# Row e of a convolution layer, spread over the partitions by GpSimd instead of by TensorE

## The chip, the cores and the metric

The kernel runs on one core of one Trainium2 chip. The metric is the device time of one execution in microseconds (us), lower is better. The engines are named as in the profile: PE is TensorE (PEld its weight loads), DVE is VectorE, ACT is ScalarE, POOL is GpSimd, SP is SyncE, which here only issues DMAs (its queue is written SPq). L1531 is line 1531 of the kernel.

## The reference

Four residual layers act in turn on an array x of 1 x 256 x 256 x 128 (height, width, channels), all in float32, each on a group-normalised x. Layer 0 is attention over rows, layers 1 and 2 are triangle multiplications, layer 3, the last, is a pair of reversible convolution blocks. Only layer 3 matters here:

```python
DN = ('NHWC', 'HWIO', 'NHWC')
def c1(t):                       # 1 x 9 taps, 128 channels -> 1 channel
    return lax.conv_general_dilated(t, w1, (1, 1), 'SAME', dimension_numbers=DN) + b1
def c2(t):                       # 128 x 128 product at each place
    return jnp.einsum('bhwc,cd->bhwd', t, w2[0, 4]) + b2
t = relu(c1(x))
y = concatenate([x[:, :1], x[:, 1:] + t[:, :-1]], axis=1)
u = relu(c1(y))
z_main = u + roll(y, 1, axis=1)
z = concatenate([z_main[:, :H-2], u[:, H-1:H] + y[:, H-2:H-1], y[:, H-1:H]], axis=1)
v = relu(c2(z))
p = concatenate([z[:, :, :1], z[:, :, 1:] + v[:, :, :-1]], axis=2)
r = relu(c2(p))
q = r + roll(p, 1, axis=2)       # with the last two columns exchanged
out = x + q
```

The first convolution c1 has one output channel. So t and u are images of 256 x 256 without channels, and z is the normalised x, moved by one row, plus an image e = u + t (moved by one row) that is the same for all 128 channels. The normalisation is r3 * x + k0 with one factor r3 and one offset k0 a channel.

## The kernel before

Data lie with channels on the 128 partitions. Layers 0 to 2 end at about 2944 us of the execution and leave x in DRAM as `x3T`. The convolution stage follows and goes in 32 steps `s` of R = 8 image rows (2048 columns, SC), with lists of work in an order written out by hand: each engine does its instructions in that order, and so does SP's DMA queue.

The image e is made ahead of the steps, by small transfers through DRAM, in 16 blocks `b` of 16 image rows (two steps):

- `taps` (L1454, L1458, L1463): six steps ahead (LEAD), TensorE multiplies x by the nine tap columns into PSUM, ScalarE copies them to `p9_st`, and four DMAs store them as nine rows of the DRAM array sD.
- `load_block` (L1473): two DMAs load the nine shifted tap rows back with the block spread over 128 partitions, one image row on 8 of them.
- `sum_taps` and `image_u` (L1493 to L1514): VectorE sums the taps to t, and forms u from t. `keep_t` (L1499) stores t to DRAM; `load_t` (L1503) loads it moved by one image row.
- `image_e` (L1519, L1521): VectorE adds u and the moved t to e, and SP stores e to DRAM (eD).
- `load_e` (L1531): four DMAs of 4 KB load e for the block's two steps into one of two tiles `p9_er`: chunk c of 512 columns goes to partition 32c for the even step and to partition 32c + 1 for the odd one.

A step `s` of the main work then is:

- `start_z(s)` (L1541): ScalarE writes r3 * x + k0, moved by one row, to the tile `p9_z` in SBUF, in one instruction of 256 columns and one of 1792.
- `finish_z(s)` (L1082, L1555): `broadcast_rows` lets TensorE multiply each chunk of row e (32 partitions) by a selector column repeated 128 times, so that all 128 partitions of two PSUM tiles hold e. VectorE adds each half (1024 columns) to z in place.
- `p_half` (L1561, L1569): TensorE multiplies z by the 128 x 128 weights, and VectorE adds the rectified product to z, giving p (`p9_pb`).
- `q_half` (L1561, L1583, L1586): the same for p, giving q. `residual` (L1575 to L1577): GpSimd adds p, moved by one column, to q, which ScalarE started as x (L1660).
- `emit` (L1598 to L1600): TensorE turns q back to tokens, ScalarE copies it from PSUM, and SP stores it.

The steps overlap. In one turn of the loop SP issues the x load of step s + 8, in odd turns the load of t and in even turns the load of e (for steps s + 2 and s + 3); then come p of step s, z of step s + 1, q of step s - 1, the residual sum of s, the image work (even turns: taps summed and t stored; odd turns: e formed and stored, then the next taps loaded), the taps of step s + 6 and the output of step s - 2. TensorE's order in a turn is therefore: product of z(s), selector products for z(s + 1), product of p(s - 1), taps of s + 6, transposes of s - 2.

PSUM is full: two tiles of two banks for the products (`p9_pm`) and two of two banks (tag "x") which the taps, the spread e and the transposes take in turn.

Of the kernel before, what the change touches and what calls it, by code (L numbers as in the profile page):

```python
# [2 lines left out]

# [5 lines left out]

F32 = mybir.dt.float32  # L10
AF = mybir.ActivationFunctionType
ALU = mybir.AluOpType
# [4 lines left out]
P = 128  # L17
N = 256
D = 128
T = N * N  # L20
SC = 2048
NSC = T // SC
CK = 512
# [9 lines left out]
def kernel(ctx: ExitStack, tc: tile.TileContext, a: dict, out: bass.AP):  # L33
    nc = tc.nc
# [28 lines left out]
    NP = N + 8  # L63
# [5 lines left out]
    eD = dram.tile([1, N * NP], F32, name="eD")  # L69
# [168 lines left out]
    with tc.tile_pool(name="x0", bufs=1) as xres, tc.tile_pool(name="p0", bufs=3) as sb:  # L238
        held = {s: xres.tile([P, SC], F32, name=f"x0_{s}") for s in range(RES, NSC)}
        with tc.tile_pool(name="p0ps", bufs=3, space=PSUM) as ps, tc.tile_pool(  # L240
            name="f0ps", bufs=2, space=PSUM
# [167 lines left out]
        with tc.tile_pool(name="p1", bufs=2) as wk_sb, tc.tile_pool(  # L409
            name="p1ps", bufs=4, space=PSUM  # L410
# [70 lines left out]
    with tc.tile_pool(name="p2e", bufs=6) as eb, tc.tile_pool(name="p2c", bufs=1) as cs:  # L481
        triT = cs.tile([P, NH, 2, N], F32, name="triT")
        with tc.tile_pool(name="p2", bufs=2) as sb, tc.tile_pool(
            name="p2S", bufs=2, space=PSUM
        ) as psS, tc.tile_pool(name="p2z", bufs=1, space=PSUM) as psZ, tc.tile_pool(
            name="p2M", bufs=3, space=PSUM
# [302 lines left out]
    xs = {}  # L789
# [58 lines left out]
    with x1_scope:  # L848
        with tc.tile_pool(name="p3", bufs=3) as sb, tc.tile_pool(
            name="p3ps", bufs=3, space=PSUM  # L850
# [41 lines left out]
        with tc.tile_pool(name="z", bufs=2) as sb, tc.tile_pool(  # L892
            name="zps", bufs=3, space=PSUM
# [21 lines left out]
            def turn_z(k):  # L915
                if k < 16:
                    return tri_turn(nc, ps, sb, AB[k // 2][0], k % 2, ident, nc.scalar.copy)
# [4 lines left out]
            at = turn_z(0)  # L922
            for k in range(16):
                nxt = turn_z(k + 1)
                pz = tri_multiply(nc, ps, at, AB[k // 2][1], k % 2).rearrange("p t n -> p (t n)")
                at = nxt
# [32 lines left out]
        with tc.tile_pool(name="p4", bufs=3) as sb, tc.tile_pool(  # L959
            name="p4psg", bufs=2, space=PSUM  # L960
        ) as psg, tc.tile_pool(name="p4psz", bufs=2, space=PSUM) as psz, tc.manual_schedule():
            zs, gts, sums = {}, {}, []
# [42 lines left out]
            for i, s in enumerate(order):  # L1005
# [14 lines left out]
                for h in range(2):  # L1020
                    hs = slice(h * 2 * CK, (h + 1) * 2 * CK)
# [5 lines left out]
                if i in by_dve:  # L1027
                    for h in range(2):
                        hs = slice(h * 2 * CK, (h + 1) * 2 * CK)
# [47 lines left out]
    def broadcast_rows(psX, rows, s, name, tag="x"):  # L1077


        rb = [psX.tile([P, 2, CK], F32, name=name, tag=tag) for _ in range(2)]  # L1080
        for c in range(4):
            nc.tensor.matmul(  # L1082
                rb[c // 2][:, c % 2, :], lhsT=sel[32 * c : 32 * c + 32, s : s + 1].to_broadcast([32, P]),
                rhs=rows[32 * c : 32 * c + 32, :], start=True, stop=True,
            )
        return [t.rearrange("p c t -> p (c t)") for t in rb]
# [9 lines left out]
    with tc.tile_pool(name="x5", bufs=7) as x5_pool, tc.tile_pool(name="p5", bufs=2) as sb, tc.tile_pool(  # L1096
        name="p5q", bufs=4
    ) as sq_pool, tc.tile_pool(name="p5psX", bufs=1, space=PSUM) as psX, tc.tile_pool(
        name="p5psM", bufs=3, space=PSUM
    ) as psM, tc.manual_schedule():  # L1100
        xs, sqs, zns, vars_ = {}, {}, {}, {}
# [81 lines left out]
        for h, rb in enumerate(broadcast_rows(psM, var, 0, "p5_pm", tag="p5_pm")):  # L1183
            hs = slice(h * H2, (h + 1) * H2)
# [7 lines left out]
        for s in range(NSC):  # L1192
            b, j = divmod(s, KB)
# [4 lines left out]
            for h in range(2):  # L1198
                hs = slice(h * H2, (h + 1) * H2)
# [51 lines left out]
    with tc.tile_pool(name="p6", bufs=3) as sb, tc.tile_pool(name="p6ps", bufs=3, space=PSUM) as ps:  # L1251
        nc.vector.memset(k1, 0.0)
        nc.gpsimd.memset(k2, 0.0)
        with tc.manual_schedule():
# [10 lines left out]
            def turn6(c):  # L1265
                return tri_turn(nc, ps, sb, quads[c // 4][0], c % 4, ident, nc.vector.tensor_copy)
# [3 lines left out]
            at = turn6(0)  # L1270
            for c in range(D):
# [5 lines left out]
                at = nxt  # L1277
# [16 lines left out]
    with tc.tile_pool(name="p7", bufs=2) as sb, tc.tile_pool(name="p7psX", bufs=2, space=PSUM) as psX, tc.tile_pool(  # L1294
        name="p7psM", bufs=2, space=PSUM
# [75 lines left out]
        for s in range(NSC):  # L1371
# [3 lines left out]
            for h in range(2):  # L1375
                hs = slice(h * H2, (h + 1) * H2)
# [30 lines left out]
    m3, r3 = gn_groups(mv3, "gn3")  # L1407
# [5 lines left out]
    k0 = const.tile([P, 1], F32, name="k0")  # L1413
# [17 lines left out]
    R = 8  # L1431
    NR = N // R
    H = R // 2
# [4 lines left out]
    with tc.tile_pool(name="p9", bufs=2) as sb, tc.tile_pool(name="p9psM", bufs=2, space=PSUM) as psM, tc.tile_pool(  # L1438
        name="p9psX", bufs=2, space=PSUM
    ) as psX, tc.manual_schedule():  # L1440
        x3r = x3T.rearrange("d (h w) -> d h w", w=N)
        xs, zs, pbs, qs, blocks = {}, {}, {}, {}, {}
        ers = [sb.tile([P, CK], F32, name=f"p9_er{i}", bufs=1) for i in range(2)]

        def load9(s):
            if s < NR:
                xs[s] = sb.tile([P, R, N], F32, name="p9_x", bufs=9)
                nc.sync.dma_start(xs[s], x3r[:, s * R : (s + 1) * R, :])

        def taps(x, h0, n):  # L1450

            pp = psX.tile([P, 2, CK], F32, name="p9_pp", tag="x")
            for c in range(n):
                nc.tensor.matmul(  # L1454
                    pp[32 * c : 32 * c + 32, 0, :], lhsT=w1f, rhs=x[:, 2 * c : 2 * c + 2, :], start=True, stop=True
                )
            st = sb.tile([P, 2, N], F32, name="p9_st", bufs=3)
            nc.scalar.activation(  # L1458
                st[0 : 32 * n].rearrange("p h w -> p (h w)"), pp[0 : 32 * n, 0, :], AF.Identity, bias=s0[0 : 32 * n]
            )  # L1460
            for c in range(n):
                at = 16 + (h0 + 2 * c + 1) * NP
                nc.sync.dma_start(  # L1463
                    sD_tap[:, at : at + 2 * NP].rearrange("k (h w) -> k h w", w=NP)[:, :, 0:N],
                    st[32 * c : 32 * c + TAPS],
                )
# [19 lines left out]
        def image_rows(d, row, n=BR):  # L1486
            return d[:, row * NP : (row + n) * NP].rearrange("o (p w) -> p (o w)", w=BW)
# [28 lines left out]
        def image_e(b):  # L1516
# [5 lines left out]
            else:  # L1522
                nc.sync.dma_start(image_rows(eD, N - BR, BR - 2), e[0 : P - 16, :])
                nc.sync.dma_start(image_rows(eD, N - 2, 1), e[P - 8 : P, :])
                nc.sync.dma_start(image_rows(eD, N - 1, 1), k["t"][P - 8 : P, 4 : 4 + BW])

        def load_e(b):

            e_chunks = eD.rearrange("o (s c h w) -> c (o s) h w", c=4, h=2, w=NP)
            for c in range(4):  # L1530
                nc.sync.dma_start(  # L1531
                    ers[b % 2][32 * c : 32 * c + 2, :].rearrange("s (h w) -> s h w", h=2),
                    e_chunks[c, 2 * b : 2 * b + 2, :, 4 : 4 + N],
                )

        def start_z(s):

            zs[s] = sb.tile([P, R, N], F32, name="p9_z", bufs=3)

            def take(lo, hi, src):  # L1540
                nc.scalar.activation(zs[s][:, lo:hi, :], src, AF.Identity, bias=k0, scale=r3)  # L1541

            take(0, 1, xs[s - 1][:, R - 1 : R, :] if s else xe[:, 1:2, :])
            if s + 1 < NR:
                take(1, R, xs[s][:, 0 : R - 1, :])
            else:
                take(1, R - 2, xs[s][:, 0 : R - 3, :])
                take(R - 2, R, xs[s][:, R - 2 : R, :])

        def finish_z(s):  # L1550
            eb = broadcast_rows(psX, ers[s // 2 % 2], s % 2, "p9_eb")
            zf = zs[s].rearrange("p h w -> p (h w)")
            for h in range(2):
                hs = slice(h * H2, (h + 1) * H2)
                nc.vector.tensor_tensor(zf[:, hs], eb[h], zf[:, hs], ALU.add)  # L1555

        def product9(src, h):
            pm = psM.tile([P, H, N], F32, name="p9_pm")
# [14 lines left out]
        def residual(s):  # L1573
            q, pb = qs[s], pbs[s]
            nc.gpsimd.tensor_tensor(q[:, :, 1 : N - 2], q[:, :, 1 : N - 2], pb[:, :, 0 : N - 3], ALU.add)  # L1575
            nc.gpsimd.tensor_tensor(q[:, :, N - 2 : N], q[:, :, N - 2 : N], pb[:, :, N - 2 : N], ALU.add)
            nc.gpsimd.tensor_tensor(q[:, :, 0:1], q[:, :, 0:1], pb[:, :, N - 1 : N], ALU.add)  # L1577
# [27 lines left out]
        nc.sync.dma_start(xe, x3r[:, N - 2 : N, :])  # L1605
        for s in range(4):
            load9(s)
        for er in ers:
            nc.gpsimd.memset(er, 0.0)
        S0 = sb.tile([P, TAPS, 2 * BW + 8], F32, name="p9_S")  # L1610
        nc.vector.memset(S0, 0.0)

# [18 lines left out]
        def begin_image(b):  # L1631
            sum_taps(b)
            keep_t(b)
            load_t(b)
# [10 lines left out]
        load_block(1)  # L1645
        for s in range(4, 8):
            load9(s)
        finish_z(0)
        for s in range(NR + 2):
            load9(s + 8)  # L1650
            b = s // 2 + 2
            if s % 2 == 1 and 2 < b < NB:
                load_t(b)
            if s % 2 == 0 and 3 < b <= NB:
                load_e(b - 1)
            if s < NR:
                pbs[s] = sb.tile([P, R, N], F32, name="p9_pb")
                nc.scalar.activation(pbs[s][:, :, 0:1], zs[s][:, :, 0:1], AF.Identity, bias=kcol[:, 0:1])
                qs[s] = sb.tile([P, R, N], F32, name="p9_q", bufs=3)
                nc.scalar.activation(qs[s], xs[s], AF.Identity, bias=kcol[:, 2:3])  # L1660
                if s + 1 < NR:
                    start_z(s + 1)
                p_half(s, 0)
                p_half(s, 1)
                del xs[s]
            if s < 2:
                begin_image(s + 1)
            if s + 1 < NR:
                finish_z(s + 1)
            if s < 2:  # L1670
                end_image(s + 1)
            if 0 < s <= NR:
                q_half(s - 1, 0)
                q_half(s - 1, 1)
                nc.scalar.activation(
                    qs[s - 1][:, :, N - 1 : N], qs[s - 1][:, :, N - 1 : N], AF.Identity, bias=kcol[:, 1:2]
                )
                del pbs[s - 1], zs[s - 1]
            if s < NR:
                residual(s)  # L1680
            if s < 2:

                for i in range(2):
                    taps(xs[4 + 2 * s + i], (4 + 2 * s + i) * R, 4)
                load_block(s + 2)
            elif b < NB:
                if s % 2 == 0:
                    sum_taps(b)
                    keep_t(b)
                    image_u(b)  # L1690
                else:
                    image_e(b)
            if s > 1 and s + LEAD < NR:
                taps(xs[s + LEAD], (s + LEAD) * R, 4)
            if s > 1 and s % 2 == 1 and b + 1 < NB:
                load_block(b + 1)
            if s > 1:
                emit(s - 2)
# [182 lines left out]
```

## Time and profile before

| | |
|---|---|
| median of 4 runs | 3387.81 us (3373.78 to 3394.29) |
| the profiled execution | 3386.14 us |
| its span (first to last instruction) | 3384.4 us |
| first row e landed, step 0 begins | 2983.9 us |
| the last product of the stage ends | 3371.5 us |
| busy share of the span: PE, DVE, ACT, POOL | 92, 67, 60, 47% |
| mean granted TensorE clock | 0.959 of full |

All rows that are shown come from the profiled execution. Busy time is time in which an engine worked on instructions; a wait is put down to the event that came last before the engine went on. In a row of the timeline the first number is the start in us from the beginning of the span, the second the time until the last of the merged instructions ended, then engine, line, operation, output <- inputs, shape and the number of instructions; square brackets hold idle time just before and what ended it. In a row of the waits stand the waiting engine and line, the releaser, the total in us, how many times, and the longest. One float32 product of 512 columns is recorded as two matmul instructions. A row of SPq is the time that SP took to issue a DMA, not the transfer.

### The profile page before, as it was taken

The page shows a single profiled execution, that of the slowest core. Times are in us where ns is not written, and L with a number is a line of the kernel's source. Part 1 is how long each engine was busy: PE and PEld are TensorE (multiplying, and loading weights), DVE is VectorE, ACT ScalarE, POOL GpSimd, SP SyncE. Part 2 cuts the span into 40 slices and gives each one's busy share as a digit, 9 for nine tenths or more (in the row PEclk, how much of TensorE's full clock was granted, in tenths as well). Part 3 has the DMA queues.
Part 4 walks back from the last instruction along what each step waited for, and adds up shares of the span by engine and source line. Part 5 has one row for each costly group of instructions (what it writes and reads, how often), then busy time and mean ns, then how long its engine had stood idle before and what let it go on. Part 6 is the DMA issues. An engine that isn't in the chain of part 4 may idle for free. (4 is left out here: it accounts for less than half of the span.)

```text
span 3384.4 us, 52577 instructions
## 1 busy us (share of the span) xinstructions
PE 3127.9 (92%) x20274; PEld 1650.7 (49%) x20274; DVE 2268.1 (67%) x2612; ACT 2018.3 (60%) x2209; POOL 1592.4 (47%) x878
## 2 busy tenths in 40 slices
PE   6669999999999999967997999999999999769998
PEld 5415555555555555524332444445999333224444
DVE  5627888888888888853555454454555777658776
ACT  3667777777777777734685444443444566636655
POOL 4046777777777777711582000002555344414444
PEclk7889999999999999989897999999999999879999
DMA  9972333333333333379597577676999898756664
GB/s 393 359 297 84 120 109 119 108 120 108 119 108 118 110 121 107 108 300 333 213 409 299 224 292 294 228 269 253 352 352 337 314 335 292 270 159 202 206 186 132
DMA packets 297977, 749.51 MB, mean 221 GB/s; under 512 B 74585, under 2 KB 145195, under 8 KB 248571
## 3 DMA queue, kind: packets, MB, share of 16 engines
q1 hardware_dynamic: 289659, 735.24, 60.1%
q0 software_dynamic: 7776, 9.81, 0.9%
q8 instruction: 162, 2.65, 0.3%
q10 hardware_dynamic: 288, 1.05, 0.1%
q14 instruction: 92, 0.75, 0.1%
HBM read 458.35 MB, written 287.64 MB: 220 GB/s over the span
## 5 line engine op out<-in xcount | busy, mean ns | idle before, releaser
L564 DVE TENSOR_TENSOR p_e<-p_S,triT 128x1024 f32<-128x1024 f32 x512 | 609.1, 1211 | 144.3 <-PE p_S L554 144.3
L574 POOL TENSOR_TENSOR p_es<-p_e 128x1024 f32<-128x1024 f32 x256 | 603.4, 2368 | 124.0 <-issue 65.4
L572 ACT ACTIVATE p_e<-p_e,mbT 128x1024 f32<-128x1024 f32 x512 | 552.0, 1138 | 59.7 <-DVE p_e L564 59.6
L1167 PE MATMUL p_pm<-p_zn,wf 128*128 128x512 f32 x1040 | 449.0, 593 | 1.9 <-ACT p_a L1202 1.9
L539 PE MATMUL p_mm<-p_xn,w 128*128 128x512 f32 x768 | 404.6, 610 | 0.3 <-DVE p_v L534 0.3
L1167 PEld LDWEIGHTS p_pm<-p_zn,wf 128*128 128x128 f32 x1040 | 196.7, 190 | 254.3 <-issue 246.6
L554 PE MATMUL p_S<-p_q,p_k 32*128 32x256 f32 x4096 | 294.9, 400 | 3.5 <-DVE p_e L564 3.2
L1575 POOL TENSOR_TENSOR p_q<-p_q,p_pb 128x2024 f32<-128x2024 f32 x32 | 144.2, 4505 | 256.3 <-DVE p_pb L1569 247.6
L554 PEld LDWEIGHTS p_S<-p_q,p_k 32*128 32x128 f32 x4096 | 185.7, 184 | 159.4 <-PE p_mm L530 91.7
L1839 PE MATMUL tp_z<-p_B,tp_at 128*128 128x256 f32 x1024 | 251.0, 388 | 0.8 <-DMA p_B<-bD 0.5
L587 PE MATMUL p_o<-p_e,p_v 128*32 128x256 f32 x4096 | 247.6, 382 | 0.0
L513 POOL TENSOR_TENSOR p_xn<-p_xn,p_rs 128x1024 f32<-128x1024 f32 x63 | 150.9, 2395 | 204.5 <-ACT p_xn L508 131.4
L1239 POOL DMA_DIRECT2D rs__17906<-rs2D x4 | 2.0, 509 | 505.8 <-DVE p_zn L1160 505.8
L1282 POOL TENSOR_TENSOR k<-k,p_sq 128x512 f32<-128x512 f32 x128 | 163.0, 1274 | 157.4 <-ACT p_sq L1280 157.4
L1392 POOL TENSOR_TENSOR p_x<-p_x,p_g 128x2048 f32<-128x2048 f32 x30 | 136.2, 4539 | 174.7 <-DVE p_g L1379 169.8
L1839 PEld LDWEIGHTS tp_z<-p_B,tp_at 128*128 128x128 f32 x1024 | 185.5, 191 | 23.0 <-DVE tp_at L1830 1.6
L539 PEld LDWEIGHTS p_mm<-p_xn,w 128*128 128x128 f32 x768 | 125.6, 190 | 104.2 <-issue 87.8
L1281 DVE TENSOR_TENSOR k<-tp_z,k 128x512 f32<-128x512 f32 x128 | 88.5, 692 | 127.7 <-ACT p_sq L1280 127.7
L587 PEld LDWEIGHTS p_o<-p_e,p_v 128*32 128x32 f32 x4096 | 120.0, 109 | 109.3 <-ACT p_g L545 41.5
L1278 ACT COPY p_K<-tp_z 128x512 f32<-128x512 f32 x128 | 74.9, 585 | 158.3 <-PE tp_z L1839 158.3
L545 ACT ACTIVATE p_g<-p_mm,bgh 128x512 f32<-128x512 f32 x128 | 88.0, 687 | 131.4 <-PE p_mm L539 131.4
L530 PEld LDWEIGHTS p_mm<-w,p_xn 128*128 128x128 f32 x1024 | 134.4, 191 | 61.1 <-issue 60.4
(379 smaller groups left out, 5909.2 us busy)
## 6 DMA issues: line engine op xcount, KB each, us to landing
p_x<-x2T SPq DMA_DIRECT2D x60, 1024.0 KB
x<-x1T SPq DMA_DIRECT2D x51, 1024.0 KB
p_x<-in_x_dram SPq DMA_DIRECT2D x32, 1024.0 KB
p_x<-xT SPq DMA_DIRECT2D x64, 512.0 KB
x2T<-x SPq DMA_DIRECT2D x32, 1024.0 KB
aD<-p_a SPq DMA_DIRECT2D x32, 1024.0 KB
bD<-p_b SPq DMA_DIRECT2D x32, 1024.0 KB
p_A<-aD SPq DMA_DIRECT2D x32, 1024.0 KB
```

The source lines that it names most:

```text
L513: nc.gpsimd.tensor_tensor(xn, xn, groups[g]["rs"], ALU.mult)
L539: nc.tensor.matmul(pm, lhsT=w, rhs=t["xn"][:, cs_], start=True, stop=True)
L554: nc.tensor.matmul(Ss[h // 2][:, h % 2, u, :], lhsT=t["k"][hp, r * N + u * P : r * N + (u + 1) * P], rhs=t["q"][hp, r * N : (r + 1) * N], ...
L564: nc.vector.tensor_tensor(e[:, :, 2 * p : 2 * p + 2, :].rearrange("p u h n -> p h u n"), Ss[p], triT[:, 2 * p : 2 * p + 2, :, :], ALU.add,)
L572: nc.scalar.activation(e[:, u, :, :], e[:, u, :, :], AF.Exp, bias=mbT[:, u, i : i + 1])
L574: nc.gpsimd.tensor_tensor(es, e[:, 0, :, :], e[:, 1, :, :], ALU.add)
L587: nc.tensor.matmul(t["o"][hp, r % 2, :], lhsT=t["v"][:, r * 2 + u, hp], rhs=e[:, u, h, :], start=(u == 0), stop=(u == 1),)
L1167: nc.tensor.matmul(pm[:, c, :], lhsT=wf2[:, i, :], rhs=zns[s][:, k * CK : (k + 1) * CK], start=True, stop=True)
L1282: nc.gpsimd.tensor_tensor(k2, k2, sq, ALU.add)
L1392: nc.gpsimd.tensor_tensor(xs7[s], xs7[s], gts[s], ALU.add)
L1575: nc.gpsimd.tensor_tensor(q[:, :, 1 : N - 2], q[:, :, 1 : N - 2], pb[:, :, 0 : N - 3], ALU.add)
L1839: nc.tensor.matmul(pz[:, t, :], lhsT=at[:, u, t * P : (t + 1) * P], rhs=Bc[:, u, :], start=(u == 0), stop=(u == 1))
```

## The change

Row e is spread over the partitions by GpSimd's partition broadcast, from SBUF to SBUF, and not by selector products on TensorE. For that

- row e of a step is loaded as a whole (2048 columns) into one partition of a single tile `p9_er`: partition 0, 32, 64 or 96 by s modulo 4. `load_e` issues two DMAs, one a step, in place of four;
- `spread_e(s)` broadcasts that partition to all 128 of a tile `p9_eb` in SBUF, which has one buffer. It is issued after `residual(s)` for step s + 2, and twice before the loop;
- ScalarE's `start_z` writes r3 * x + k0 not into the z tile but into two PSUM tiles of tag "x", in three instructions (256, 768 and 1024 columns), and VectorE's sum reads PSUM and `p9_eb` and writes z;
- the two MEMSETs of `p9_er` go, and a GpSimd library that holds the broadcast is loaded in their place;
- `p9_st` has two buffers in place of three.

```diff
-        ers = [sb.tile([P, CK], F32, name=f"p9_er{i}", bufs=1) for i in range(2)]
+        er = sb.tile([P, SC], F32, name="p9_er", bufs=1)
+        ebs, zps = {}, {}
...
-            st = sb.tile([P, 2, N], F32, name="p9_st", bufs=3)
+            st = sb.tile([P, 2, N], F32, name="p9_st")
...
+        def row_e(s):
+            at = 32 * (s % 4)
+            return er[at : at + 1, :]
+
         def load_e(b):
-            e_chunks = eD.rearrange("o (s c h w) -> c (o s) h w", c=4, h=2, w=NP)
-            for c in range(4):
+            for s in range(2 * b, 2 * b + 2):
                 nc.sync.dma_start(
-                    ers[b % 2][32 * c : 32 * c + 2, :].rearrange("s (h w) -> s h w", h=2),
-                    e_chunks[c, 2 * b : 2 * b + 2, :, 4 : 4 + N],
+                    row_e(s).rearrange("o (h w) -> o h w", w=N),
+                    eD.rearrange("o (h w) -> o h w", w=NP)[:, s * R : (s + 1) * R, 4 : 4 + N],
                 )
+        def spread_e(s):
+            if s < NR:
+                ebs[s] = sb.tile([P, SC], F32, name="p9_eb", bufs=1)
+                nc.gpsimd.partition_broadcast(ebs[s], row_e(s))
+
         def start_z(s):
-            zs[s] = sb.tile([P, R, N], F32, name="p9_z", bufs=3)
-            def take(lo, hi, src):
-                nc.scalar.activation(zs[s][:, lo:hi, :], src, AF.Identity, bias=k0, scale=r3)
+            zps[s] = [psX.tile([P, H, N], F32, name="p9_zp", tag="x") for _ in range(2)]
+            def take(lo, hi, src):
+                h = lo // H
+                nc.scalar.activation(zps[s][h][:, lo - h * H : hi - h * H, :], src, AF.Identity, bias=k0, scale=r3)
             take(0, 1, xs[s - 1][:, R - 1 : R, :] if s else xe[:, 1:2, :])
+            take(1, H, xs[s][:, 0 : H - 1, :])
             if s + 1 < NR:
-                take(1, R, xs[s][:, 0 : R - 1, :])
+                take(H, R, xs[s][:, H - 1 : R - 1, :])
...
         def finish_z(s):
-            eb = broadcast_rows(psX, ers[s // 2 % 2], s % 2, "p9_eb")
-            zf = zs[s].rearrange("p h w -> p (h w)")
-            for h in range(2):
+            zs[s] = sb.tile([P, R, N], F32, name="p9_z", bufs=3)
+            zf, eb = zs[s].rearrange("p h w -> p (h w)"), ebs.pop(s)
+            for h, zp in enumerate(zps.pop(s)):
                 hs = slice(h * H2, (h + 1) * H2)
-                nc.vector.tensor_tensor(zf[:, hs], eb[h], zf[:, hs], ALU.add)
+                nc.vector.tensor_tensor(zf[:, hs], zp.rearrange("p h w -> p (h w)"), eb[:, hs], ALU.add)
...
-        for er in ers:
-            nc.gpsimd.memset(er, 0.0)
+        nc.gpsimd.load_library(library_config.all_libraries[10])
...
+        spread_e(0)
         finish_z(0)
+        spread_e(1)
         for s in range(NR + 2):
...
                 residual(s)
+                spread_e(s + 2)
```

More of the change, by code (lines that the diff above doesn't have):

```diff
@@ L5 @@
 import concourse.tile as tile
-from concourse import mybir
+from concourse import library_config, mybir
 from concourse.masks import make_identity
@@ L1543, in start_z @@
             take(0, 1, xs[s - 1][:, R - 1 : R, :] if s else xe[:, 1:2, :])
+            take(1, H, xs[s][:, 0 : H - 1, :])
             if s + 1 < NR:
-                take(1, R, xs[s][:, 0 : R - 1, :])
+                take(H, R, xs[s][:, H - 1 : R - 1, :])
             else:
-                take(1, R - 2, xs[s][:, 0 : R - 3, :])
+                take(H, R - 2, xs[s][:, H - 1 : R - 3, :])
                 take(R - 2, R, xs[s][:, R - 2 : R, :])
         def finish_z(s):
-            eb = broadcast_rows(psX, ers[s // 2 % 2], s % 2, "p9_eb")
```

## The prediction

> **What bounds the kernel now.** I read the totals first, then the chain that ended last, then the timeline of the convolution stage engine by engine, then the waits of the DMA queue.
>
> ```profile
> span 3384.4 us, 52577 instructions
> PE 3127.9 (92%) x20274; PEld 1650.7 (49%) x20274; DVE 2268.1 (67%) x2612; ACT 2018.3 (60%) x2209; POOL 1592.4 (47%) x878
> ...
> 3050.00:3073.00 23.00, 23.00 (x100) 10.47 (x99) 17.98 (x24) 15.27 (x18) 9.76 (x6) 1.00 0.71 208
> ```
>
> The last row is a window of the stage: its length, then the busy time of PE, weight loads, DVE, ACT and POOL, the granted clock, the DMA share and GB/s. TensorE is the busy engine: 92% of the program, and in the window 3050 to 3073 of the stage 23.00 of 23.00 us, at clock 1.00. This invites the reading "TensorE bounds the stage, so each product removed is time won". The timeline of TensorE says what one step is and where that reading ends:
>
> ```profile
> 3049.84 3.60 PE L1561 MATMUL p_pm<-p_z,w2c 128*128 128x512 f32 x8
> 3053.38 1.14 PE L1082 MATMUL p_eb<-p_er,sel 32*128 32x512 f32 x8
> 3054.45 3.70 PE L1561 MATMUL p_pm<-p_pb,w2c 128*128 128x512 f32 x8
> 3058.07 1.07 PE L1454 MATMUL p_pp<-p_x,w1f 128*32 128x512 f32 x8
> 3059.07 1.97 PE L1598 MATMUL p_pt<-ident,p_q 128*128 128x128 f32 x16
> 3060.88 3.60 PE L1561 MATMUL p_pm<-p_z,w2c 128*128 128x512 f32 x8
> ...
> 3087.56 1.55 PE L1082 MATMUL p_eb<-p_er,sel 32*128 32x512 f32 x8 [1.01 <-DMA p_er<-eD]
> ```
>
> A step is 11.04 us (3060.88 - 3049.84), of which the selector products take 1.07 (3054.45 - 3053.38). But from 3087 on, TensorE waits in most second steps for row e itself. The waits of SP's queue and its rows around that moment show who sets the row's time:
>
> ```profile
> SPq L1521 <- DVE p_e L1519: 59.7, 11, 6.6
> SPq L1463 <- DMA p_x<-x3T: 20.5, 10, 2.9
> ...
> 3078.99 2.43 SPq L1448 DMA_DIRECT2D p_x<-x3T  x1
> 3081.46 2.05 SPq L1531 DMA_DIRECT2D p_er<-eD  x4
> 3084.78 3.08 SPq L1463 DMA_DIRECT2D sD<-p_st  x4
> 3087.95 0.41 SPq L1600 DMA_DIRECT2D out_dram<-p_o  x1
> 3088.40 1.88 SPq L1448 DMA_DIRECT2D p_x<-x3T  x1
> 3090.38 1.18 SPq L1503 DMA_DIRECT2D p_t<-tD  x1
> ...
> 3096.49 0.20 DVE L1519 TENSOR_TENSOR p_e<-p_u,p_t 128x33 f32<-128x33 f32 x1 [2.30 <-DMA p_t<-tD]
> ```
>
> This is a loop. VectorE forms e (L1519) when t has landed; SP, which waited for that 59.7 us in 11 times, stores e, then issues in order the taps, the tap loads, an output, the x load and the load of row e; the row lands with the x load ahead of it; the last tap stores of the next step wait for that x load (20.5 us, 10 times); behind them stand the next output, x load and load of t; t lands, and VectorE can form the next e. The stores of e at 3050.03 and 3286.00 lie ten pairs of steps apart: 23.60 us a pair, against 22.07 for TensorE's two steps. So from about 3050 to 3276 the stage goes by this SP-and-DMA loop; TensorE bounds it only after the last wait for a row (3276).
>
> **The change part by part.** All against the profiled execution, 3386.14 us (span 3384.4); the median of the runs shown is 1.7 higher.
>
> *Selector products away.* 31 steps lose 1.07 us of TensorE. In the loop-bound stretch this is worth nothing by itself: the cover is the loop, and TensorE merely waits longer. In the tail, from the wait at 3276.14 to the end, TensorE is the chain: one product of 2.51 and seven of 1.07, 10.0 us. Not all comes: rows 28 and 30 are issued until 3318.2 and 3336.0 and were used at 3322.64 and 3343.07, so they allow some 2 and 4 us, after the longer broadcast. I take 5 us.
>
> *Row e loaded by two DMAs in place of four.* SP's 2.05 us (1.10, then 0.26 to 0.28 each) become about 1.4. The gain is hidden by the wait for the x load, but the count matters. The issues carry eight completion semaphores in turn, and the third tap store, eighth behind the x load, is the one that waited until 3087.22. With two issues fewer, the output stands in that place and all four tap stores go before the wait: 3087.22 to 3087.95, 0.73 us a pair, 10 pairs: 7.3 us.
>
> *Broadcast on POOL, X us each, 32 times.* No row shows it. Bounds: four MEMSETs of 128x512 (542 ns) make 2.17, a copy of 128x512 (627 ns) times four 2.51 with its fixed part counted four times (a 128x16 sum takes 0.23, so 1.9 without three of them), a two-operand sum of 128x2048 4.54. It reads one row and writes one stream, so it is nearest to memset and copy: X = 2.2, ends 1.9 and 4.54. POOL then has 4.96 + 2.2 = 7.2 of 11.04 us; it does not become the bound.
>
> *Who waits behind it.* On POOL the broadcast of row e+2 waits for the row's landing L; the residual sum of the next step (4505 + 232 + 222 ns) is queued behind, then the broadcast of row e+3. The residual's reader, the transposes, comes two steps later, so that costs nothing. But POOL work also holds VectorE:
>
> ```profile
> 2995.25 4.46 POOL L1575 TENSOR_TENSOR p_q<-p_q,p_pb 128x2024 f32<-128x2024 f32 x1 [38.02 <-DVE p_pb L1569]
> ...
> 2996.37 3.40 DVE L1495 SCALAR_TENSOR_TENSOR p_t<-p_acc,b,p_in 128x41 f32<-128x41 f32 x1
> ```
>
> L1495 reads two SBUF tensors, has a median of 0.263 us and here took 3.40, to the end of POOL's sum; L1569, with one operand in PSUM, kept its 1.28 beside such sums. L1519 also reads two SBUF tensors, and it is in the loop. POOL is busy until L + 0.1 + X + 5.0 + 0.1 + X = L + 9.6; t lands at L + 8.9, 9.9, 10.6 and 11.2 in the four pairs where both ends can be read (the products' start after a wait for the row, and L1519's start), 10.1 on average, 9.4 with the 0.73. So L1519 is held 0.2 us a pair. The loop wins 0.73 - 0.2 = 0.5 a pair, 5 us over ten.
>
> [...] The trace shows the hold only for POOL sums. [...]
>
> *ScalarE.* z in 256, 768 and 1024 columns into PSUM in place of 256 and 1792 into SBUF. From 593 ns (256) and 1872 (1792), 0.833 ns a column: 593 + 1020 + 1233 = 2.85 for 2.47, +0.38 a step. No row writes PSUM from ScalarE; ends: a copy of 1024 columns at 1015 (no dearer than before) and twice this step. ScalarE idles 3.57 us a step before L1458, which covers all of it. The first half is ready about 0.6 us earlier than the whole was, and VectorE's 0.71 us wait for ScalarE goes; inside the loop that is worth nothing. The PSUM tiles take the places of the former ones; the one written first is freed by ScalarE's own copies.
>
> *VectorE.* The sum still has one PSUM and one SBUF operand: 1218 ns, unchanged. A late row now stops VectorE's sum rather than TensorE; after L the sum starts at 2.3 us, before at 1.44 (3088.87 - 3087.43). The second product goes on meanwhile, which is where the tail's 5 us come from.
>
> *Start.* Two MEMSETs (1.0 us) leave, a library load enters. POOL is free from 2943.7 to the first row at 2983.9: 40 us of cover; below that it costs nothing, beyond it one for one. The first sum followed the row by 2.3 us before (2986.16 - 2983.89) and follows by 2.3 now: 0. The buffer of one broadcast and two instead of three tap buffers bind nothing: each is reused a step, or two, after its reader.
>
> Sum: -5 (loop) - 5 (tail) + 0 = -10: 3376 from the profiled execution, 3378 from the median; I say 3377.
>
> **The rivals.** *TensorE's full share comes* (if the loop loses as much as TensorE, say because t lands sooner): 31 x 1.07 = 33 us, 3353. For it: 92% and the full window. Against it: TensorE's waits for rows and 23.60 against 22.07. *POOL holds e* (other side): the same chain with X = 4.54 ends at L + 14.2, 4.8 us after t; less 0.73, ten pairs: +41, 3427 with the tail's gain gone. For it: the 3.40 us row; against: the memset and copy rows. It passes 0.5% when the hold reaches 2.4 us a pair, X = 3.3. *The library load outlasts its cover*: a load of 60 us gives +20 - 10, 3396. Nothing in the trace prices it. *The change moves the wait only*: rows land later as each goes whole into one partition; 1 us a pair undoes both gains, 3386.
>
> **How the numbers follow.** 0.5% is 17 us, about what can be told from no change. Forecast 0.46 (3377, own range 3366 to 3394); full TensorE share 0.20; POOL holds e 0.20; library 0.07; wait moved only 0.07. Faster by over 0.5%: the 0.20 and 0.05 of the forecast's lower edge, 0.25. Slower: POOL's 0.20, most of the library's, 0.26. Same 0.49. The range takes in 3353 below and, above, X up to 3.3 (3403) and the library: 3350 to 3408; left out is the worse half of POOL's case and scraps.
>
> **What would show it.** L1082 in the stage gone and TensorE's step without waits near 9.97; the pairs of e stores still near 23 us (loop right) or near 20 (TensorE right); broadcasts of 1.9 to 2.5 us; L1519 longer than 0.2, or starting as POOL ends (hold right); L1463 no longer waiting for the x load and L1600 doing so (count right); the first broadcast within 0.2 us of its row (library covered). A broadcast over 3.3 us, or a loop that has another waiter than I named, makes me wrong.

## The result and the profile after

| | before | after |
|---|---|---|
| median | 3381.65 us (72 runs) | 3395.28 us (46 runs) |
| ratio | 1 | 1.0039, 95% interval 1.0027 to 1.0050 |
| the profiled execution | 3386.14 us | 3388.24 us |
| convolution stage in it, from the issue of its first load (xe) to the end | 428.3 us | 436.8 us |

The changed kernel is slower by 13 us. The forecast was 10 us faster. The two profiled executions differ by only 2 us: near the end of layer 2 of the one before, VectorE waits six times for a load of x, 12.4 us in all, and in the one after it doesn't. So the stage is compared, not the span. Lines after 1454 have moved: the taps are L1455, their copies L1459 and stores L1464, `image_e` L1520, its store L1522, the broadcast L1543, z into PSUM L1551, VectorE's sum L1566, the products L1572, p L1580, the transposes L1609, the output L1611.

The totals, and the window 3050 to 3073 (its length, busy PE, weight loads, DVE, ACT, POOL, clock, DMA share, GB/s):

```profile
span 3386.5 us, 52060 instructions
PE 3085.8 (91%) x20018; PEld 1637.5 (48%) x20018; DVE 2279.8 (67%) x2612; ACT 2030.2 (60%) x2241; POOL 1666.6 (49%) x908
...
3050.00:3073.00 23.00, 20.34 (x85) 9.65 (x88) 17.76 (x24) 15.05 (x18) 13.70 (x9) 1.00 0.70 207
```

TensorE is no longer full: 20.34 of 23.00 us instead of 23.00, at the same clock. Yet the time did not fall. Its timeline:

```profile
3052.97 3.60 PE L1572 MATMUL p_pm<-p_z,w2c 128*128 128x512 f32 x8
3056.40 3.60 PE L1572 MATMUL p_pm<-p_pb,w2c 128*128 128x512 f32 x8
3059.93 1.06 PE L1455 MATMUL p_pp<-p_x,w1f 128*32 128x512 f32 x8
3060.93 1.97 PE L1609 MATMUL p_pt<-ident,p_q 128*128 128x128 f32 x16
3062.73 3.60 PE L1572 MATMUL p_pm<-p_z,w2c 128*128 128x512 f32 x8
3067.40 3.70 PE L1572 MATMUL p_pm<-p_pb,w2c 128*128 128x512 f32 x8 [1.07 <-DVE p_pb L1580]
3072.69 1.06 PE L1455 MATMUL p_pp<-p_x,w1f 128*32 128x512 f32 x8 [1.59 <-DVE p_z L1566]
```

The first step takes 9.76 us (3062.73 - 3052.97; forecast 9.97), the next has waits on VectorE. What TensorE no longer does, it now waits. SP's waits of the loop, from 3050 to 3290:

```profile
SPq L1522 <- DVE p_e L1520: 66.2, 11, 6.3
SPq L1611 <- DMA p_x<-x3T: 20.1, 10, 3.0
```

The output L1611, now the eighth DMA behind the x load, has taken the place of the tap stores (20.1 us in 10 waits; they waited 20.5 before), as the count of the DMAs foretold. The broadcast on POOL, and one pair of steps around it, POOL and then VectorE:

```profile
L1543 POOL PARTITION_BROADCAST p_eb<-p_er x32 | 73.5, 2297 | 134.4 <-DMA p_er<-eD 98.7 <-ACT p_zp L1551 12.7 <-ACT p_q L1687 12.6
```

```profile
3093.05 2.29 POOL L1543 PARTITION_BROADCAST p_eb<-p_er  x1 [6.98 <-DMA p_er<-eD]
3095.20 4.63 POOL L1586 TENSOR_TENSOR p_q<-p_q,p_pb 128x2024 f32<-128x2024 f32 x1
3099.67 0.34 POOL L1587 TENSOR_TENSOR p_q<-p_q,p_pb 128x16 f32<-128x16 f32 x1
3099.86 0.34 POOL L1588 TENSOR_TENSOR p_q<-p_q,p_pb 128x8 f32<-128x8 f32 x1
3100.29 2.29 POOL L1543 PARTITION_BROADCAST p_eb<-p_er  x1
...
3101.20 1.28 DVE L1520 TENSOR_TENSOR p_e<-p_u,p_t 128x33 f32<-128x33 f32 x1 [0.84 <-DMA p_t<-tD]
```

A broadcast takes 2.30 us (forecast 2.2). The second one of a pair runs to 3102.58, and L1520, which took 0.20 us before, takes 1.28 and ends at 3102.48, as the broadcast ends. So the broadcast held it for 1.08 us, as POOL's sum held L1495 in the kernel before.

**Where the stage lost.** At its start. The time from the first xe load to the fourth store of e was 93.9 us and is 105.3. First the profile before, then after, both around the taps of steps 2 and 3:

```profile
2966.53 1.06 PE L1454 MATMUL p_pp<-p_x,w1f 128*32 128x512 f32 x8 [0.73 <-DMA p_x<-x3T]
2969.20 1.94 PE L1454 MATMUL p_pp<-p_x,w1f 128*32 128x512 f32 x8 [1.60 <-DMA p_x<-x3T]
...
2980.79 0.32 SPq L1521 DMA_DIRECT2D eD<-p_e  x1
2983.48 2.80 SPq L1463 DMA_DIRECT2D sD<-p_st  x8
...
3007.84 0.20 DVE L1519 TENSOR_TENSOR p_e<-p_u,p_t 128x33 f32<-128x33 f32 x1 [4.20 <-DMA p_t<-tD]
```

```profile
2962.94 0.69 ACT L1459 ACTIVATE p_st<-p_pp,s 128x512 f32<-128x512 f32 x1 [5.09 <-DMA sD<-p_st]
2963.52 0.56 ACT L1551 ACTIVATE p_zp<-p_xe,k,gn_rstd 128x256 f32<-128x256 f32 x1
2964.12 2.12 ACT L1551 ACTIVATE p_zp<-p_x,k,gn_rstd 128x768 f32<-128x768 f32 x2
...
2975.82 0.32 SPq L1522 DMA_DIRECT2D eD<-p_e  x1
...
2982.39 2.35 DVE L1566 TENSOR_TENSOR p_z<-p_zp,p_eb 128x1024 f32<-128x1024 f32 x2 [6.60 <-POOL p_eb L1543]
2983.72 3.29 PE L1455 MATMUL p_pp<-p_x,w1f 128*32 128x512 f32 x16 [24.20 <-DVE p_z L1566]
2986.42 2.83 SPq L1464 DMA_DIRECT2D sD<-p_st  x8
...
3010.06 0.20 DVE L1520 TENSOR_TENSOR p_e<-p_u,p_t 128x33 f32<-128x33 f32 x1 [9.53 <-DMA p_t<-tD]
```

Before, step 0's z went to SBUF, and TensorE made the taps of steps 2 and 3 in the two PSUM tiles of tag "x" while the first e was still being made. Now ScalarE writes z(0) into those two tiles at 2963.5, and VectorE frees them only when the spread row 0 has come (2982.4). The taps wait 24.2 us for that. Their stores leave SP 10.6 us after the first store of e (2986.42 - 2975.82), before 2.7 after it (2983.48 - 2980.79), and what stands behind them in the queue comes later: the second store of e follows the first by 34.5 us instead of 27.3. The first row shows the third buffer of the taps missed too: ScalarE waited 5.09 us for a tap store (the first store of e came 1.5 us later after the xe load).

### The profile page after: what moved, and what is told of

It reads as the page before. It is cut to its first block, busy times and chain, and to the rows that moved or that the text cites. A ratio compares the mean times of both kernels' runs of the same rounds, so it can differ in the third digit from the quotient of the medians.

```text
span 3386.5 us, 52060 instructions
## 1 busy us (share of the span) xinstructions
PE 3085.8 (91%) x20018; PEld 1637.5 (48%) x20018; DVE 2279.8 (67%) x2612; ACT 2030.2 (60%) x2241; POOL 1666.6 (49%) x908
## 3 DMA queue, kind: packets, MB, share of 16 engines
q10 hardware_dynamic: 288, 1.05, 0.1%
```

## The experiments

Three parts of the stage serve as measures: *start* (first xe load to the fourth store of e), *ten pairs* (fourth to fourteenth store) and *tail* (fourteenth store to the end). Each comes from the one profiled execution of each kernel. The spread can be read from kernels with the same stage: the one before, and the three that only add or put back a library, have ten pairs of 236.0, 240.4, 239.3 and 238.7 us, so up to 4.4 us there is nothing. Ratios are to the kernel before, on the same chip.

| kernel | start | ten pairs | tail | stage | ratio (95%) |
|---|---|---|---|---|---|
| before | 93.9 | 236.0 | 98.4 | 428.3 | 1 |
| after | 105.3 | 234.5 | 97.0 | 436.8 | 1.0039 (1.0027 to 1.0050) |
| z(0) after the taps | 98.5 | 237.3 | 97.0 | 432.8 | 1.0013 (0.9989 to 1.0036) |
| before + library | 93.6 | 240.4 | 97.7 | 431.7 | 1.0015 (0.9993 to 1.0036) |
| the same again | 94.4 | 239.3 | 95.9 | 429.6 | 1.0016 (0.9994 to 1.0037) |
| before + two row loads | 94.5 | 232.7 | 96.4 | 423.6 | 0.9981 (0.9959 to 1.0003) |
| the same again | 92.5 | 229.8 | 94.9 | 417.2 | 0.9986 (0.9967 to 1.0005) |
| broadcast behind e | 104.3 | 228.1 | 96.3 | 428.7 | 1.0028 (1.0006 to 1.0050) |
| three repairs | 95.5 | 229.5 | 94.7 | 419.7 | 0.9993 (0.9976 to 1.0010) |
| before, selector doubled | 94.1 | 239.6 | 95.7 | 429.3 | 0.9988 (0.9975 to 1.0001) |
| before + library, put back | 92.2 | 238.7 | 95.4 | 426.2 | 1.0006 (0.9985 to 1.0027) |
| three repairs, put back | 95.7 | 227.1 | 96.2 | 419.0 | 0.9990 (0.9978 to 1.0002) |
| after, put back | 105.9 | 238.9 | 94.8 | 439.6 | 1.0041 (1.0024 to 1.0058) |

### Step 0's z after the taps

```diff
-        start_z(0)
         load_taps(S0, N - 1, 1, BW, BW + 4, P - 8)
...
+        start_z(0)
         spread_e(0)
         finish_z(0)
```

> The changed kernel with one move: z of step 0 is written to PSUM after the taps of steps 2 and 3, not before. Theory A (at the start the two PSUM tiles of z(0) are held until row 0 has come, the taps of steps 2 and 3 wait for them, their stores come 8 us later on SP, and five x loads and the store of t behind them too): the second store of e follows the first by about 27 us instead of 34.5, the stage (first load of its edge rows to the end) goes from 436.8 to about 429, and the kernel from 13 us slower than before to about 5 us slower. Theory B (the loss is in the main stretch, where POOL holds the sum that forms e): the start may move, but the end does not, still 13 us slower.

The second store of e follows the first by 27.5 us (34.5 in the changed kernel, 27.3 before), and the start falls from 105.3 to 98.5 us; the kernel lies 0.26% below the changed one, about as much as the two intervals together leave open. That the early write into the shared PSUM tiles held the taps is shown. The start is still 4.6 us longer than before.

### The library alone, in the kernel before

```diff
+        nc.gpsimd.load_library(library_config.all_libraries[10])
```

> The kernel before, and the GpSimd library loaded where the changed kernel loads it; nothing uses it. Theory A2 (a program that leaves another library behind pays at its own start: GpSimd's first mask comes 9.8 us later in the changed kernel, and all that follows 5 to 8 us later): 5 to 8 us slower than before, with the first mask at 11 us instead of 1.2. Theory B (the load is covered): no difference, within 2 us.

> The kernel before with the library's load added and nothing that uses it (the same kernel as in the first call, for a narrower interval). Theory (the first masks of the program wait 9.8 us, of which about 5 reach the end): ratio about 1.0015, first mask of the program at 11 us instead of 1.2. Rival (the wait is made up in the layers before this one): ratio 1.000.

The stage doesn't change, but the program's first mask does. The timeline of POOL in the kernel before, and in the first of these two runs:

```profile
1.21 0.29 POOL masks.py:199 TENSOR_SCALAR_AFFINE_SELECT ident<-ident 128x128 f32<-128x128 f32 x1
```

```profile
11.24 0.28 POOL masks.py:199 TENSOR_SCALAR_AFFINE_SELECT ident<-ident 128x128 f32<-128x128 f32 x1 [10.09 <-issue]
```

POOL waits 10.1 us for something that no row names; in the changed kernel it waits 9.8, 2.97 ms before the first broadcast. Both ratios together (their mean; its half-width is half the root of the sum of the two half-widths' squares) are 1.0016, 1.0000 to 1.0031: some 5 us, barely apart from none.

### Two loads for a pair of rows, in the kernel before

```diff
-            for c in range(4):
+            for s in range(2):
+                at = (2 * b + s) * R
                 nc.sync.dma_start(
-                    ers[b % 2][32 * c : 32 * c + 2, :].rearrange("s (h w) -> s h w", h=2),
-                    e_chunks[c, 2 * b : 2 * b + 2, :, 4 : 4 + N],
+                    ers[b % 2].rearrange("(c q) t -> q c t", q=32)[s].rearrange("c (h w) -> c h w", h=2),
+                    eD.rearrange("o (h w) -> o h w", w=NP)[:, at : at + R, 4 : 4 + N].rearrange(
+                        "o (c h) w -> (o c) h w", h=2
+                    ),
                 )
```

> The kernel before, with row e loaded by two DMAs (one for each step, four pieces of 2 KB) in place of four; all else as before, selector products too. The prediction's count term alone: the last tap stores go before the wait for the x load, the loop is 0.7 us a pair shorter, about 7 us faster. If the loop is paced by how long the x load takes to land and not by SP's order behind it: no difference.

> The kernel before, where each load of two rows of e is two transfers, one per step, instead of four (the same kernel as in the first call, for a narrower interval). Theory (each DMA less per pair frees SP and one completion semaphore, 0.3 to 0.4 us a transfer): ratio 0.997 to 0.999, ten pairs about 232.7. Rival (the first result was the spread of the runs): ratio 1.000.

Only the number of DMAs changes; selector products and tiles stay. Ten pairs take 232.7 and 229.8 us, against a mean of 238.6 over the four kernels with the old loads: 7.4 us less. SP's waits in the second run, 3050 to 3290:

```profile
SPq L1521 <- DVE p_e L1519: 53.3, 10, 5.8
SPq L1499 <- DVE p_t L1496: 20.0, 11, 3.1
SPq L1473 <- DMA sD<-p_st: 11.9, 14, 1.5
SPq L1602 <- DMA p_x<-x3T: 8.9, 7, 1.8
```

The wait of the tap stores for the x load (20.5 us) is gone, and the output (L1602) waits 8.9 us in its place. Both ratios together are 0.9984, 0.9969 to 0.9998, worked out as above: this small part of the change, by itself, is faster than the changed kernel. Against the kernel before, the ratio alone proves little: the kernel with doubled selector products, which only adds work, has 0.9988. The ten pairs are the evidence, and with them the timing inside a pair: from one store of e the next sum of e starts 22.9 us later on average over both runs, in the four kernels with the old loads 23.6.

### The broadcast behind e

```diff
+        def spread_after_e(s):
+            mark = sb.tile([P, 1], F32, name="p9_mark")
+            nc.gpsimd.tensor_copy(mark, e_of[0][:, 0:1])
+            spread_e(s)
...
-                spread_e(s + 2)
+                if s % 2 == 0 or s < 2 or b >= NB:
+                    spread_e(s + 2)
...
                     image_e(b)
+                    spread_after_e(s + 2)
```

> The changed kernel, but in odd steps from 3 to 27 the broadcast for step s + 2 stands behind the forming of e (a copy of one column of e on GpSimd stands before it and waits for e). Theory C (the broadcast holds the sum that forms e, 1.0 us longer in each pair of steps, and the loop with it): that sum takes 0.2 us again, the pairs go from 23.4 to about 22.4 us, 10 us faster than the changed kernel, some 3 us slower than before. Theory A (only the start counts): the sum is shorter but the pairs stay near 23.4 and the time where it was, 13 us slower than before.

The copy of one column of e (0.19 us) makes the second broadcast of a pair start behind L1520. L1520 takes 0.20 us again in every block, and ten pairs take 228.1 us; with the two later kernels that have this edit, 228.2 on average. The changed kernel's two profiles have 236.7 on average. So the hold costs 8.5 us over ten pairs, and the rows say the same: L1520 lasts 1.05 us on average between the fourth and the fourteenth store, 0.85 more than without a hold. The start, which the edit reaches only in its last steps, still takes 104.3 us. The ratio, 1.0028, is not clearly apart from 1.0039; the span of this profile, 3411.6 us, is 25 us longer than the changed kernel's while its stage is shorter, so only its stage is used.

### The three repairs together

The two edits above (the column of e now copied into an existing tile), and

```diff
-            st = sb.tile([P, 2, N], F32, name="p9_st")
+            st = sb.tile([P, 2, N], F32, name="p9_st", bufs=3)
...
-            k["u"] = sb.tile([P, BW], F32, name="p9_u")
+            k["u"] = sb.tile([P, BW], F32, name="p9_u", bufs=1)
```

> The changed kernel with the three repairs together: the ScalarE part of step 0's z written after the taps of steps 2 and 3, the broadcast of the odd steps issued behind row block e's sum (a one-column GpSimd copy of e holds it back), and three buffers for the tap tiles (one for u, to make room). Theory (z(0)'s PSUM tiles, the tap buffers and the hold of e cost the time, the library's load stays): stage from the first xe load to the end about 420 us (436.8 changed, 428.3 before): first to second store of e about 27.3 as before, first store of e about 24.7 after the xe load, ten pairs about 229 as in the run with the broadcast behind e. Against the kernel before: ratio 0.997 to 1.000 with the library's 5 us still paid at the start of the program. Rival (the broadcast itself, ready 2.3 us later than a selector product would be, costs in each step): ten pairs at 234 or more, ratio 1.002 or more. Rival (the gains of the two repairs overlap, since both only advance the same SP queue): ratio about 1.001.

The timeline of the start (the PE rows are the taps of steps 1 to 3):

```profile
2958.66 1.54 PE L1455 MATMUL p_pp<-p_x,w1f 128*32 128x512 f32 x8 [0.64 <-DMA p_x<-x3T]
2961.15 1.06 PE L1455 MATMUL p_pp<-p_x,w1f 128*32 128x512 f32 x8 [0.95 <-DMA p_x<-x3T]
2963.70 1.07 PE L1455 MATMUL p_pp<-p_x,w1f 128*32 128x512 f32 x8 [1.49 <-DMA p_x<-x3T]
2965.46 0.56 ACT L1558 ACTIVATE p_zp<-p_xe,k,gn_rstd 128x256 f32<-128x256 f32 x1
```

The taps wait for x only, and z(0) comes after them. The first store of e is 24.75 us after the xe load (26.1 changed, 24.7 before), so the third tap buffer is worth its 1.5 us; ten pairs take 229.5. The stage is 17 us shorter than the changed one's and 8.6 shorter than before, and the time 0.46% below the changed kernel's. The rival that the broadcast itself costs in each step is out. The other rival, that the gains overlap (1.001), is just at the end of the interval; the start and the ten pairs, which each gained what the single edits gave, speak against it. Against the kernel before, what the stage won shows only in part (0.9993).

### The selector products doubled

```diff
-        for c in range(4):
+        for c in [c for c in range(4) for _ in range(times)]:
...
-            eb = broadcast_rows(psX, ers[s // 2 % 2], s % 2, "p9_eb")
+            eb = broadcast_rows(psX, ers[s // 2 % 2], s % 2, "p9_eb", times=2 if 4 <= s <= 23 else 1)
```

> The kernel before with the selector products of steps 4 to 23 issued twice into the same PSUM tile (20 x 4 products more of 64 columns' worth of the same work; the result is the same). My theory, by which the loop is held by SP and the transfers behind e at 23.6 us a pair and TensorE needs 22.1: TensorE goes to about 24.2 a pair, so the ten pairs take about 6 us more (242), ratio about 1.002. Rival (TensorE is the bound and the products cost their full share): 20 x 1.07 = 21 us more, ratio about 1.006. Third (they fit beside the waits wholly): 0 to 1 us more.

```profile
3053.35 3.60 PE L1561 MATMUL p_pm<-p_z,w2c 128*128 128x512 f32 x8
3056.88 2.02 PE L1082 MATMUL p_eb<-p_er,sel 32*128 32x512 f32 x16
3058.83 3.70 PE L1561 MATMUL p_pm<-p_pb,w2c 128*128 128x512 f32 x8
3062.46 1.06 PE L1454 MATMUL p_pp<-p_x,w1f 128*32 128x512 f32 x8
3063.45 1.97 PE L1598 MATMUL p_pt<-ident,p_q 128*128 128x128 f32 x16
3065.26 3.60 PE L1561 MATMUL p_pm<-p_z,w2c 128*128 128x512 f32 x8
```

Four products of 512 columns are added in each of the 20 steps. TensorE's step is 11.91 us now, without waits, and the ten pairs take 239.6, within the 236.0 to 240.4 of the same loop without the extra products. The ratio excludes the +21 us of a TensorE-bound stage (1.006). It excludes the 6 us that I gave, too: the products fit beside the waits, but only just. TensorE is now busy for all of the 240 us from 3050 to 3290 (230.55 before), and two steps at 11.91 make 23.82 of the 23.96 us that a pair takes. This fits what is seen from the other side: the stage is 420.4 us (mean of two) with two row loads and the products, and 419.4 with three repairs and no products.

### The standard library put back

One more instruction at the end of the stage, in the kernel before with the library, in the changed kernel, and in the one with three repairs:

```diff
             if s > 1:
                 emit(s - 2)
+        nc.gpsimd.load_library(library_config.standard)
```

> The kernel before with the library's load added and, as GpSimd's last instruction of the program, the standard library loaded again. Theory (the 9.8 us before the first mask are the standard library's load, which the program asks for at its start and which costs nothing when it is still resident from the execution before): first mask at 1.2 us again, ratio 1.000 (0.9985 to 1.0015). Rival (a program that names two libraries pays at its start whatever was resident): first mask at 11 us, ratio 1.0015.

> The changed kernel with only the standard library loaded again at the end. Theory (about 5 of the 13 us slower come from the start of the program, the rest from the stage): ratio 1.002 to 1.003, first mask at 1.2 us, stage about 437 us. Rival (the whole loss is in the stage): 1.0039 still.

> The changed kernel with the three repairs (step 0's z written after the taps of steps 2 and 3, odd broadcasts behind row block e, three tap buffers) and the standard library loaded again at the end. Theory: the 0.9993 of the three repairs less the library's 0.0015, so 0.997 to 0.9985, first mask at 1.2 us, stage about 420 us. Rival (the start's wait is swallowed by the layers between): the same 0.9993 as without.

POOL's timeline in the first of the three (the same row stands in the other two):

```profile
1.45 0.29 POOL masks.py:199 TENSOR_SCALAR_AFFINE_SELECT ident<-ident 128x128 f32<-128x128 f32 x1 [0.29 <-POOL ones L77]
```

The 10 us at the start are gone: the first mask starts at 1.45 us in the three kernels that end with the standard library, at 10.96 in the changed kernel and at 11.24 in the one before with the library alone. That the 10 us are the loading of the standard library is the likely reading; no row names it. The rival, that naming two libraries costs whatever is resident, is out. What this is worth at the end of the program isn't settled, and the 5 us that I expected did not show. The changed kernel did not gain (1.0041, where I had 1.002 to 1.003), the repaired one gained 0.03% (0.9990, where I had 0.9985 at most), the kernel before with the library 0.1%, all within the intervals. So the slower time is not carried by the library. And even repaired, the kernel with the broadcast is not told apart from the one before: its interval ends at 1.0002.

## Why the prediction was wrong

**The step that failed is "Start: 0".** It compared two ends: the first sum follows row 0 by 2.3 us, as before. That held (2982.39 - 2980.05 = 2.34). But it did not ask what else takes turns in the PSUM tiles that z(0) now fills. The sentence "the PSUM tiles take the places of the former ones" is true in the loop, where taps, z and transposes already alternate; at the start z(0) is written before the taps of steps 2 and 3, and is held until the first e. It cost 11.4 us in the profiled pair, and 12.1 as the mean of the changed kernel's two profiles against the mean of the four with the old stage. Of these, moving z(0) gave back 6.9; the "two instead of three tap buffers", which I said "bind nothing", account for 1.5 at the first store of e. About 2 us remain after all repairs (95.6 against 93.5). The profile of the three repairs shows them as the same hold of VectorE by broadcasts, in the first steps, where the repair doesn't move the broadcasts: L1514 takes 1.54 us at 3017.58 and L1496 1.06 at 3033.96, where they take 0.20 and 0.26 when free, 2.1 us together.

**The selector products, worth nothing in the loop: right.** Pairs stayed near 23.5 us though TensorE's step fell to 9.76, and doubling the products cost nothing beyond the spread. The full-share rival (-33 us) is out.

**The DMA count, 7.3 us: right**, by itself 7.4 us, and the wait went where the count said. That the sizes agree so closely is luck, as ten pairs of the same stage differ by up to 4.4 us between profiles. The run shows which queue carries the loop.

**The hold of e, 0.2 us a pair: mis-sized; it is 0.85.** The mechanism and POOL's side were right: POOL is busy until 9.53 us after the first broadcast starts (forecast 9.6 after the row). But I put t's arrival at 9.4 after the row, and L1520 starts 8.45 after the first broadcast on average (8.15 to 9.22 in the ten blocks). Both ends moved. Counted from one store of e, L1520 starts after 22.4 and 22.8 us in the changed kernel's two profiles, and the same sum after 23.4 to 23.8 in the four kernels with the old loads: t comes about 1 us sooner, not 0.73. The first broadcast starts after 13.9 and 14.3, and TensorE, where it waited for the row, went on after 13.4 to 13.8: the row is used about half a us later. With two loads and no broadcast that was 13.8 and 14.3 too, so the single partition is not needed to explain it. The hold ate what the count won: the loop's -5 became -1.9 (236.7 against 238.6), within the spread. The rival "POOL holds e" named this mechanism, but by a broadcast of 4.54 us; it is 2.30.

**The broadcast's price, 2.2 us: right** (2.30). The four memsets, 2.17, were the nearest of its bounds.

**The tail, 5 us: wrong.** It won 1.4 us in the profiled pair, and nothing beyond the spread over all (95.9 against 96.8). I counted when rows were ready, but not what the broadcasts do to VectorE, nor that VectorE's work had been covered by the selector products. Its image sums, which also read two SBUF tensors, stand ahead of p in its order. First VectorE, then TensorE, in the changed kernel:

```profile
3300.72 1.66 DVE L1514 TENSOR_TENSOR p_u<-p_u,p_acc 128x33 f32<-128x33 f32 x1
3302.41 0.24 DVE L1515 TENSOR_SCALAR p_u<-p_u,b 128x33 f32<-128x33 f32 x1
3302.57 2.46 DVE L1580 SCALAR_TENSOR_TENSOR p_pb<-p_pm,kcol,p_z 128x1020 f32<-128x1020 f32 x2
...
3303.89 5.40 PE L1572 MATMUL p_pm<-p_pb,w2c 128*128 128x512 f32 x8 [2.54 <-DVE p_pb L1580]
```

L1514, 0.20 us when free, lasts until the broadcast of 3300.18 to 3302.47 ends; then comes p, for which TensorE waits 2.54 us. The same happens before 3327.80, where L1496 is held (1.59 us for 0.26) and TensorE waits 3.35. The holds are 2.8 us of these 5.9; the rest is VectorE's other work that stands ahead of p. The product after each of the two waits then takes 5.40 us in place of 3.60, at a mean granted clock of 0.68 against 1.00 from 3312 to 3319: 3.6 us more. So waits for VectorE and slower products behind them took what TensorE had gained.

**The library: its cover in the stage held, its price was elsewhere.** The first broadcast ran when its row landed, after 42.8 idle us of POOL. I looked for the load's price where it is written; what goes with the library is the wait of 9.8 us before the first mask, which is gone (0.29) where the standard library is loaded again at the end.

Together, over the profiles: start +12.1 (forecast 0), ten pairs -1.9 (forecast -5), tail -0.9 (forecast -5): +9.3 us in the stage, of the 13 measured. The rest lies within the intervals; the library's start may have part in it.

## What to carry to other kernels

Before an intermediate moves into a shared pool of buffers, list at the start of the stage, where the order differs from the loop, who takes the next buffers and when the new holder lets go: here an early write to PSUM cost 6.9 us, and the loop won 1.9. The broadcast on GpSimd was also priced by the short VectorE instructions that it held (L1520 took 1.05 us on average for 0.20); where one of these is in the loop, try the GpSimd work behind it, which took 8.5 us off ten pairs here. And where a stage goes by a DMA queue as this one did, look at the number of transfers: two loads fewer a pair, with all else as before, took 7.4 us off ten pairs.

## What the runs showed of the hardware

Of the kernels that load another GpSimd library and leave it loaded, the changed one starts POOL's first mask at 10.96 us, after a wait of 9.8, and the kernel before with the library alone at 11.24, after 10.1; the kernel before starts it at 1.21. Where the standard library is loaded again at the end, the first mask starts at 1.45. The wait stands before that mask and not at the first broadcast, which started when its row landed. What fills it, no row names.
